# The last product of an attention takes over the tokens without neighbours, and an expert's result takes its weight and bias in one pass

## The chip, the cores and the metric

The kernel runs on one NeuronCore of a Trainium2 chip. The metric is the device time of one execution in microseconds (us); the figures given are medians of three runs. The engines are named as in the profile: PE (TensorE matmul), PEld (TensorE weight load), DVE (VectorE), ACT (ScalarE), POOL (GpSimd), SP (SyncE, which here issues DMAs).

## The reference

Two layers of a graph network on 2708 tokens of 256 numbers, with a 0/1 matrix `adj` of 2708 x 2708. Each layer is an attention over neighbours and a mixture of eight experts of which every token uses two, both with a residual:

```python
x = x + gnn0(layernorm(x), adj)     # masked softmax(q k' / 16) v, then elu
x = x + ffn0(layernorm(x))          # top 2 of 8 experts, hidden 1024, gelu
x = x + gnn1(layernorm(x), adj)     # below
x = x + ffn1(layernorm(x))          # top 2 of 8 experts, hidden 512, gelu

def gnn1(X, A):
    H = X @ W_fc + b_fc
    scores = (H @ w_att[:256])[:, None] + (H @ w_att[256:])[None, :] + b_att
    alpha = softmax(where(A > 0, scores, -1e9), axis=1)
    return alpha @ H
```

In `gnn1` the term of the row cancels in the softmax, so a token's result is a sum of `exp(s_k) * H_k` over its neighbours k, divided by the sum of `exp(s_k)`. A token without any neighbour gets, by the softmax of equal numbers, the plain mean over all 2708 tokens: the sum of all `H_k` divided by 2708. The same holds for layer 0.

## The kernel before

**Stages.** The profiled execution runs attention 0 (to about 525 us), the 45 chunks of experts 0 (to 863 us), attention 1 (to 1044 us), the 47 chunks of experts 1 (to 1255 us), and a tail that reads the experts' two results per token back and writes the output. Tokens lie in 22 tiles: 21 of 128 rows and one of 20 (`NT`, `ROWS`, `TAIL` = 20). Four tiles make a block of 512 (`GROUP` = 4, `QUARTER` = 32).

**Attention 1** (`layer1_attention`). The tiles of queries are taken in groups of 6, 6, 4, 3 and 3 (`GROUPS`), each tile with a PSUM accumulator (`acc`, six buffers). In a group a loop goes over the tiles of keys, k = 0 to 21. For k < 21, `attend` multiplies the 0/1 mask (`m`, turned from one-byte to four-byte numbers by ACT two steps ahead, L685) with the keys' weighted values in two parts (`parts`, L713). For k = 21, the 20 last keys, the masks of four tiles lie one under another on the partitions in quarters of 32, and `tails` (a copy by ACT in `load_tails`, L676) is multiplied with `e_tail` (L719). In the first group (`keys_and_values`) the values are computed on the way (L641), with PE kept busy by 28 products of no use before it starts (`busy(PAUSE)`, L752).

After a group, `evict` copies each accumulator to `raw` in SBUF, DVE and ACT in turn (L739), and gives the tile's further work to a `Line`. A line starts a new tile every `gap` of its steps and lets every running tile do one step, that is, one piece up to its next `yield`. In attention 1 a step comes after each k, or after every second k in the groups of 3. Pieces of one tile: `over_sum` (L244 to L249: is the sum of weights zero, a sum of N in its place, reciprocal, add the sum of all values where it was zero); residual, logits and the statistics of the norm, whose power -0.5 POOL computes (L727, L730, L209 to L215); the normed row, twice in memory, as `row0` and `row1` of DROW = 258 numbers, with the token's number behind it (POOL, L959); the best two experts and their one-hot (L992 to L1013); an exponential by ACT (L1015); two small products that count places (L1018, L1019); the two weights and places (L1022 to L1035), and two indirect DMAs by POOL that scatter the rows to `disp` (L1038). Layer 0 has the same `route` with some differences. The sum of all values, `total`, comes from `all_sum` after the first group (L819, L231, L234, L238).

Order of work: in attention 1 and experts 1 PE, ACT and DVE run in the order in which the code issues them (`manual_schedule`); POOL is ordered by the code in the first group of attention 1, SP everywhere. In layer 0 a planner orders the instructions of PE, ACT, DVE and POOL.

**Experts** (`slots`). For every chunk of 128 rows: `turned` (rows onto columns, L1247, then xe by DVE in layer 0, L1251, by ACT in layer 1, L1257); `up` (a copy `bias2` of the output bias, L1263, by DVE in layer 0 and ACT in layer 1; products L1270; gelu by ACT, L1278); `down` of the chunk before (products L1286; `y` = product + bias2, L1292; `y` times the row's weight, L1293; an indirect DMA by POOL into `xd`, which adds in layer 0, L1304, and only writes in layer 1, L1297). Between the products of `down` and `y`, `fetch` issues what the chunk three places later needs: its weights by an indirect DMA of POOL (L1199) and its rows by a DMA of SP (L1214). A row of weights already in place is given an index out of bounds and nothing is moved. In layer 0 an adding DMA past chunk 24 waits until the one before has landed. After chunk 44 (`OFTEN` = 45) the number of chunks is read and further ones run behind a branch (L1361, L1368).

The line goes on in experts 1 with two steps a chunk: the last tiles of attention 1 are routed there.

Of the kernel before, what the change touches and what calls it, by code (L numbers as in the profile page):

```python
# [9 lines left out]
F32 = mybir.dt.float32  # L10
I32 = mybir.dt.int32
# [26 lines left out]
assert TAIL <= QUARTER  # L38
# [31 lines left out]
def adj_ffn_kernel(ctx: ExitStack, tc: tile.TileContext, a: dict, out: bass.AP):  # L70
# [170 lines left out]
    def over_sum(raw, r, n, total):  # L241

        z = small.tile([P, 3], F32, name="z")
        nc.vector.tensor_scalar(z[:r, 0:1], raw[:r, n : n + 1], 0.0, None, ALU.is_equal)  # L244
        nc.vector.scalar_tensor_tensor(
            z[:r, 1:2], z[:r, 0:1], float(N), raw[:r, n : n + 1], op0=ALU.mult, op1=ALU.add
        )
        nc.vector.reciprocal(z[:r, 2:3], z[:r, 1:2])
        nc.vector.scalar_tensor_tensor(  # L249
            raw[:r, :n], total[:r], z[:r, 0:1], raw[:r, :n], op0=ALU.mult, op1=ALU.add  # L250
        )
        return z[:r, 2:3]
# [47 lines left out]
    def layer0_attention(line):  # L300
        with ExitStack() as scope, ExitStack() as until_last:
# [207 lines left out]
            def finish(t, raw, total):  # L509
                r, xr = ROWS[t], xin.pop(t)  # L510
                rinv = over_sum(raw, r, D, total)
                nc.vector.scalar_tensor_tensor(
                    raw[:r, :D], raw[:r, :D], rinv, bv_b[:r], op0=ALU.mult, op1=ALU.add
                )
                neg = rows0.tile([P, D], F32, name="neg", bufs=2)
                nc.vector.tensor_scalar(neg[:r], raw[:r, :D], 0.0, None, ALU.min)
                nc.scalar.activation(neg[:r], neg[:r], AF.Exp)
                yield
                nc.vector.scalar_tensor_tensor(
                    neg[:r], neg[:r], -1.0, raw[:r, :D], op0=ALU.add, op1=ALU.max  # L520
                )
                x1 = rows0.tile([P, D], F32, name="x1")
                nc.vector.tensor_add(x1[:r], neg[:r], xr[:r])
                yield from experts0.route(t, x1)
# [78 lines left out]
    def layer1_attention(mTs, kept, line, first_masks):  # L603
        with ExitStack() as scope:
# [63 lines left out]

            tails, converted_last = {}, [None]

            def load_tails(ts_):

                tails.clear()
                for b in sorted({t // GROUP for t in ts_}):
                    tails[b] = pool.tile([P, P], F32, name="m_tail")
                    nc.scalar.copy(tails[b], mTs[b][:, NT - 1, :P])  # L676
# [28 lines left out]
            def attend(ts_, k, accs):  # L705
                if k == GROUP:
                    load_tails(ts_)
                masks = next(masks_of_keys) if k < NT - 1 else None
                for t, acc in zip(ts_, accs):
                    r, j = ROWS[t], t % GROUP  # L710
                    if masks:
                        for i in range(2):
                            nc.tensor.matmul(  # L713
                                acc[:r], masks[t], parts[:, k, i],
                                start=(k == 0 and i == 0), stop=False,
                            )
                        continue
                    keys = slice(j * QUARTER, j * QUARTER + TAIL)
                    nc.tensor.matmul(  # L719
                        acc[:r, : VALUES + 1], tails[t // GROUP][keys, :r], e_tail[keys], start=False, stop=True  # L720
                    )

            def finish(t, raw, total):
                r, x2 = ROWS[t], kept[:, t]
                rinv = over_sum(raw, r, VALUES, total)
                yield
# [9 lines left out]
            def evict(ts_, accs, total):  # L736
                for j, (t, acc) in enumerate(zip(ts_, accs)):
                    raw = rows.tile([P, VALUES + 1], F32, name="raw", bufs=6)
                    (nc.scalar.copy if j % 2 else nc.vector.tensor_copy)(  # L739
                        raw[: ROWS[t]], acc[: ROWS[t], : VALUES + 1]  # L740
                    )
                    line.add(finish(t, raw, total))

            def keys_and_values(ts_, accs):
# [14 lines left out]
                for i in range(-3, NT + LAG1 - 1):  # L759
                    if i + 3 < NT:  # L760
                        stats[i + 3] = norm_begin(i + 3)
# [14 lines left out]
                    if 0 <= i < NT:  # L776
                        nc.vector.tensor_reduce(
                            sums_of[:, :, i], xT.pop(i)[:, :, : ROWS[i]], AX.X, ALU.add
                        )

# [4 lines left out]
            g0, total, beginning = 0, None, None  # L785
            for g, wide in enumerate(GROUPS):
# [30 lines left out]
                if g == 0:  # L817
                    sums = pool.tile([P, DC], F32, name="sums", bufs=1)
                    nc.vector.tensor_reduce(sums, sums_of, AX.X, ALU.add)  # L819
                    total = all_sum(pool, sums, wfc, VALUES, "total1")  # L820
# [3 lines left out]
                evict(ts_, accs, total)  # L824
# [42 lines left out]
    class Experts:  # L867
# [64 lines left out]
        def route(self, t, x, logits=None):  # L932
# [5 lines left out]
            rows2 = [  # L938
                routing.tile([P, DROW], F32, name=f"row{j}") if own_norm
                else kept_pool.tile([P, DROW], F32, name=f"row{j}", bufs=6)  # L940
                for j in range(2)
            ]
# [8 lines left out]
            if own_norm:  # L951
                xt = rows.tile([P, D], F32, name="xn", bufs=4)[:r]
                normed(xt, x[:r], mean, once)
                normed(rows2[0][:r, :D], x[:r], mean, twice)
            else:
                xt = rows2[0][:r, :D]
                row = normed(xt, x[:r], mean, once)
            for j in range(2):
                index = nc.gpsimd.tensor_copy(  # L959
                    rows2[j].bitcast(I32)[:r, D : D + 1],  # L960
                    token[:r, 0 if own_norm else j, t : t + 1],
                )
                if not own_norm:

                    tc.add_manual_dep(
                        index.ins, row.ins.name,
                        mybir.DependencyInfo(
                            mybir.DependencyClass.Sync, mybir.DependencyReason.DATA
                        ),
                        reason="no sooner than the row",  # L970
                    )
            if own_norm:
                nc.vector.tensor_copy(rows2[1][:r, :D], rows2[0][:r, :D])
            yield
            if not own_norm:
                (nc.vector.tensor_copy if self.begun else nc.scalar.copy)(
                    rows2[1][:r, :D], rows2[0][:r, :D]
# [45 lines left out]
            for j in range(2):  # L1023
                nc.vector.tensor_scalar(
                    rows2[j][:r, D + 1 : D + 2], p[:r, j : j + 1], den[:r, 1:2], None, ALU.mult
                )
# [9 lines left out]
            for j in range(2):  # L1036
# [3 lines left out]
                        rows2[j][:r], None,  # L1040
# [156 lines left out]
        def fetch_weights(self, s):  # L1197
            w, packed = self.ring[s % RING], self.packed_weights[0]
            nc.gpsimd.indirect_dma_start(  # L1199
# [3 lines left out]
            )  # L1203
            return w
# [34 lines left out]
        def slots(self, two, ps_mm, ps_tp, ps_acc, line):  # L1239
# [20 lines left out]
            def up(w, xe):  # L1260

                bias2 = two.tile([P, D], F32, name="bias2", bufs=2 if own_norm else 4)
                (nc.vector.tensor_copy if own_norm else nc.scalar.copy)(bias2, w[:, b2:b1])  # L1263
# [19 lines left out]
            def down(s, w, xg, hT, bias2, then):  # L1283
# [8 lines left out]
                nc.vector.tensor_add(y, ps, bias2)  # L1292
                nc.vector.tensor_scalar(y, y, xg[:, D + 1 : D + 2], None, ALU.mult)  # L1293
# [13 lines left out]
                if s < FULL_AFTER[self.early]:  # L1307
                    tc.declare_no_dep(start.ins, group=self.groups[3], reason="other rows of xd")
                    tc.add_to_no_dep_group(self.groups[2], start.ins)

# [5 lines left out]
            def slot(s, s1):  # L1316
# [4 lines left out]
                hT, bias2 = up(w, xe)  # L1321
# [5 lines left out]
                def fetch():  # L1327
# [4 lines left out]
                    if s + AHEAD < SLOTS and s + AHEAD == len(self.fetched):  # L1332
                        self.fetched.append((self.fetch_weights(s + AHEAD), self.fetch_rows(s + AHEAD)))
# [7 lines left out]
                if behind is None:  # L1341
                    fetch()
                else:
# [121 lines left out]
```

## Time and profile before

| what | value |
|---|---|
| median of three runs | 1288.06 us (1287.43 to 1289.81) |
| the profiled execution's own time | 1287.64 us |
| its span, first to last instruction | 1285.9 us |
| PE busy | 1200.1 us |
| DVE, ACT, POOL busy | 551.0, 439.9, 420.2 us |

The profile is of one execution. Its rows give start and duration of instructions in us from the span's start; in a row, brackets hold the idle time of the engine before it and what ended it. "sum, times, longest" stands in the view of waits. In the view by stage each engine's busy time in a stretch is followed by the number of instructions, and PEclk is the share of the TensorE clock that was granted.

### The profile page before, as it was taken

How to read it: one execution, taken by the hardware profiler on the slowest of the kernel's cores; microseconds unless marked ns; L12 is line 12 of the kernel's file. 1: busy time of each engine (PE TensorE's matmuls, PEld its weight loads, DVE VectorE, ACT ScalarE, POOL GpSimd, SP SyncE). 2: the span in 40 equal slices, each digit the busy share in tenths (PEclk: the TensorE clock that was granted, in tenths of full speed). 3: DMA queues.
4: the chain of work that ended last, by engine and by line, in shares of the span. 5: the costliest groups of instructions: out<-in, count | busy, mean ns of one | idle time of the engine just before them, and what ended most of it. 6: DMA issues, size and time to landing. Idle time of an engine off the chain costs nothing. (4 is left out here: it accounts for less than half of the span.)

```text
span 1285.9 us, 20986 instructions
## 1 busy us (share of the span) xinstructions
PE 1200.1 (93%) x7136; PEld 967.9 (75%) x7136; DVE 551.0 (43%) x2087; ACT 439.9 (34%) x1301; POOL 420.2 (33%) x538
## 2 busy tenths in 40 slices
PE   7999999999999999899999999999999888799980
PEld 4776666566656666699999999988998877799870
DVE  6623843633634526541212212116867775222114
ACT  3222222122112212433233232325766546444430
POOL 4100110110120113243333343335635457455550
PEclk9999999999999999999999999999999979899995
DMA  8701364997955905456657845433005125544358
GB/s 268 227 1 64 111 180 120 248 245 169 257 136 136 194 23 234 182 159 176 200 156 254 298 120 175 110 100 89 2 18 197 44 58 194 159 141 147 122 177 263
DMA packets 107242, 197.83 MB, mean 154 GB/s; under 512 B 26753, under 2 KB 81718, under 8 KB 100986
## 3 DMA queue, kind: packets, MB, share of 16 engines
q1 hardware_dynamic: 77276, 110.09, 30.8%
q0 software_dynamic: 27040, 83.56, 20.6%
q10 hardware_dynamic: 2814, 2.77, 0.7%
q8 instruction: 59, 0.97, 0.3%
q14 instruction: 53, 0.43, 0.1%
HBM read 263.63 MB, written 66.12 MB: 256 GB/s over the span
## 5 line engine op out<-in xcount | busy, mean ns | idle before, releaser
L1270 PE MATMUL mm<-xe,ring 128*128 128x128 f32 x2192 | 274.4, 279 | 17.7 <-ACT xe L1257 12.6
L1270 PEld LDWEIGHTS mm<-xe,ring 128*128 128x128 f32 x2192 | 264.9, 194 | 33.1 <-ACT xe L1257 14.9
L1286 PE MATMUL acc<-ring,hT 128*128 128x256 f32 x1096 | 267.7, 382 | 4.7 <-ACT hT L1278 3.0
L1278 ACT ACTIVATE hT<-mm,ring 128x128 f32<-128x128 f32 x548 | 156.5, 369 | 295.9 <-issue 191.9
L1286 PEld LDWEIGHTS acc<-ring,hT 128*128 128x128 f32 x1096 | 196.0, 192 | 25.7 <-ACT hT L1278 3.6
L504 PE MATMUL acc<-v,p 128*128 128x257 f32 (+1 forms) x880 | 209.1, 389 | 0.0
L447 PE MATMUL s<-g,xnT 128*128 128x512 f32 x420 | 206.3, 606 | 2.4 <-DVE mT L459 2.3
L1292 DVE TENSOR_TENSOR y<-acc,bias 128x256 f32<-128x256 f32 x92 | 39.0, 424 | 367.2 <-PE acc L1286 349.3
L504 PEld LDWEIGHTS acc<-v,p 128*128 128x128 f32 (+1 forms) x880 | 153.3, 190 | 18.1 <-issue 0.8
L1199 POOL DMA_INDIRECT ring<-L_ffn_packed,weight_row x98 | 103.4, 1055 | 183.0 <-issue 101.5
L1038 POOL DMA_INDIRECT disp<-row,to x88 | 88.2, 1002 | 147.6 <-issue 52.8
L713 PE MATMUL acc<-parts,m 128*128 128x266 f32 x924 | 130.5, 300 | 1.5 <-DVE raw L739 1.1
L215 POOL TENSOR_TENSOR ln_rs<-ln_rs,minus_half 128x2 f32<-128x2 f32 x88 | 66.5, 758 | 195.1 <-DVE ln_rs L211 175.9
L459 DVE TENSOR_SCALAR mT<-s 128x512 fp8e4<-128x512 f32 x105 | 71.9, 687 | 131.2 <-ACT p L458 131.1
L713 PEld LDWEIGHTS acc<-parts,m 128*128 128x128 f32 x924 | 120.5, 191 | 7.7 <-ACT m L685 2.6
L458 ACT ACTIVATE p<-s 128x512 f32<-128x512 f32 x105 | 62.1, 595 | 165.1 <-PE s L453 164.2
L447 PEld LDWEIGHTS s<-g,xnT 128*128 128x128 f32 x420 | 75.4, 191 | 49.0 <-issue 41.9
L1304 POOL DMA_INDIRECT xd<-y,xg x45 | 71.1, 1580 | 88.6 <-issue 32.2
L453 PEld LDWEIGHTS <-apart 128*128 128x128 fp8e4 x420 | 32.7, 99 | 61.2 <-issue 61.2
L685 ACT CAST m<-mT 128x512 fp32r<-128x512 fp8e4 (+4 forms) x168 | 71.0, 472 | 9.0 <-PE acc L713 6.3
L334 DVE TENSOR_SCALAR apart<-adj 128x677 fp8e4<-128x677 int32 x80 | 40.7, 511 | 53.1 <-DMA adj<-in_adj_dram 52.6
L1297 POOL DMA_INDIRECT xd<-y,xg x47 | 47.3, 1007 | 24.8 <-PE tp L1247 9.1
(228 smaller groups left out, 1154.5 us busy)
## 6 DMA issues: line engine op xcount, KB each, us to landing
adj<-in_adj_dram SPq DMA_DIRECT2D x84, 338.5 KB
L_ffn_packed<-in_L_ffn_W_dram SPq DMA_DIRECT2D x16, 1024.0 KB
xg<-disp SPq DMA_DIRECT2D x98, 129.0 KB
L_ffn_packed<-in_L_ffn_W_dram SPq DMA_DIRECT2D x16, 512.0 KB
neighbours<-mT SPq DMA_DIRECT2D x5, 1408.0 KB
mT<-neighbours SPq DMA_DIRECT2D x5, 1408.0 KB
xin<-in_x_dram SPq DMA_DIRECT2D x42, 128.0 KB
ring<-L_ffn_packed SPq DMA_DIRECT2D x4, 1154.0 KB
```

Source lines behind the costliest of these rows:

```text
L215: nc.gpsimd.tensor_tensor(rs[:r, 1], rs[:r, 0], minus_half[:r], ALU.pow)
L447: nc.tensor.matmul(ps[:kr, :nb], xnT[:, c, k0 : k0 + kr], g[:, c, :nb], start=(c == 0), stop=False,)
L459: nc.vector.tensor_scalar(mT[:kr, k, :], ps[:kr, :nb], -BIG / 2, None, ALU.is_gt, saturate=False,)
L504: nc.tensor.matmul(accs[j][:r], p[keys, q0 : q0 + r], v[keys, k, :], start=(k == 0), stop=(k == NT - 1),)
L685: nc.scalar.copy(m[:, : q1 - q0], mTs[b][:, k, q0 - b * BN : q1 - b * BN])
L713: nc.tensor.matmul(acc[:r], masks[t], parts[:, k, i], start=(k == 0 and i == 0), stop=False,)
L1038: nc.gpsimd.indirect_dma_start(disp[:], bass.IndirectOffsetOnAxis(ap=to[:r, j : j + 1], axis=0), rows2[j][:r], None,)
L1199: nc.gpsimd.indirect_dma_start(w, None, packed[:], bass.IndirectOffsetOnAxis(ap=self.weight_row[:, s : s + 1], axis=0), bounds_check=E * P ...
L1270: nc.tensor.matmul(ps[:, i, :], w[:, c * hidden + f * P : c * hidden + (f + 1) * P], xe[:, c, :], start=(c == 0), stop=(c == DC - 1),)
L1278: nc.scalar.activation(hT[:, f, :], ps[:, i, :], AF.Gelu, bias=w[:, b1 + f : b1 + f + 1])
L1286: nc.tensor.matmul(ps, hT[:, f, :], w[:, w2 + f * D : w2 + (f + 1) * D], start=(f == 0), stop=(f == hc - 1),)
L1304: start = nc.gpsimd.indirect_dma_start(xd[:], at, y, None, bounds_check=N - 1, oob_is_err=False, compute_op=ALU.add)
```

## The change

Six things change.

1. **Tokens without neighbours.** Layer 0 leaves for each tile a column of 0/1 in `alone` (1 where the token has no neighbour). In attention 1 `over_sum` is gone: the last product gets one more key, row 20 of each quarter. Its mask is `alone`, its value the sum of all values, its weight N. The columns are copied into `rows_alone` (DVE, `load_alone`, at k = 0), turned by PE (a transpose into a buffer of `misc`) and joined to the tail masks by DVE in `load_tails` at k = 4, in place of ACT's copy. `place`, nine small DVE operations, makes the two 0/1 columns that say which partitions are keys and which the one behind. The sum of all values is computed in `sum_of_all` inside the first group, and added to `e_tail` by two DVE operations. `finish` takes the reciprocal alone and has one `yield` fewer.
2. **Evictions of attention 1.** ACT takes the first two of three, DVE the third.
3. **Two rows in one tile.** `row0` and `row1` become `row[:, 0]` and `row[:, 1]`. In layer 1 one POOL copy writes both token numbers (two before); in both layers one DVE operation writes both weights (two before).
4. **Scaled bias.** `bias2` is the bias times the row's weight, made in `up`; `y` is then one DVE operation, product times weight plus `bias2`.
5. **Layer 0, chunk 44.** `down` of chunk 43 is issued whole, and the fetch for chunk 47 after it; the weights' DMA on POOL waits until the adding DMA has landed.
6. `over_sum` in layer 0 writes its 0/1 column to `alone` instead of a column of `z`.

```diff
+    alone = const.tile([P, NT], F32, name="alone")
+    nc.gpsimd.memset(alone, 0.0)
-    def over_sum(raw, r, n, total):
+    def over_sum(raw, r, n, total, alone):
-        nc.vector.tensor_scalar(z[:r, 0:1], raw[:r, n : n + 1], 0.0, None, ALU.is_equal)
+        nc.vector.tensor_scalar(alone, raw[:r, n : n + 1], 0.0, None, ALU.is_equal)
...
+            place = pool.tile([P, 4], F32, name="place", bufs=1)
+            in_tail, behind_tail = place[:, 2:3], place[:, 3:4]
...
+            rows_alone = [
+                pool.tile([P, P], F32, name=f"alone{i}", bufs=1) for i in range(DC)
+            ]
+            for x in rows_alone:
+                nc.gpsimd.memset(x, 0.0)
+            def load_alone(ts_):
+                for b in sorted({t // GROUP for t in ts_}):
+                    n = len(BLOCKS[b][2])
+                    nc.vector.tensor_copy(
+                        rows_alone[b % DC].rearrange("p (j n) -> p j n", j=GROUP)[:, :n, TAIL],
+                        alone[:, b * GROUP : b * GROUP + n],
+                    )
             def load_tails(ts_):
...
-                    nc.scalar.copy(tails[b], mTs[b][:, NT - 1, :P])
+                    ps = misc.tile([P, GROUP, P], F32, name="misc")
+                    nc.tensor.transpose(ps[:, 0, :], rows_alone[b % DC], ident)
+                    nc.vector.scalar_tensor_tensor(
+                        tails[b], mTs[b][:, NT - 1, :P], in_tail, ps[:, 0, :],
+                        op0=ALU.mult, op1=ALU.add,
+                    )
...
-                    keys = slice(j * QUARTER, j * QUARTER + TAIL)
+                    keys = slice(j * QUARTER, j * QUARTER + TAIL + 1)
...
-            def finish(t, raw, total):
+            def finish(t, raw):
                 r, x2 = ROWS[t], kept[:, t]
-                rinv = over_sum(raw, r, VALUES, total)
-                yield
+                z = small.tile([P, 2], F32, name="z")
+                rinv = z[:r, 1:2]
+                nc.vector.reciprocal(rinv, raw[:r, VALUES : VALUES + 1])
...
-                    (nc.scalar.copy if j % 2 else nc.vector.tensor_copy)(
+                    (nc.vector.tensor_copy if j % 3 == 2 else nc.scalar.copy)(
...
+            def sum_of_all():
+                ps = misc.tile([P, GROUP, P], F32, name="misc").rearrange("p g n -> p (g n)")
+                for c in range(DC):
+                    nc.tensor.matmul(
+                        ps[:, :VALUES], sums_wide[:, c, :], wfc[:, c, :VALUES],
+                        start=(c == 0), stop=(c == DC - 1),
+                    )
+                nc.vector.scalar_tensor_tensor(
+                    e_tail[:, :VALUES], ps[:, :VALUES], behind_tail, e_tail[:, :VALUES],
+                    op0=ALU.mult, op1=ALU.add,
+                )
...
                 for i in range(-3, NT + LAG1 - 1):
+                    if i == NT:
+                        sum_of_all()
...
-                    sums = pool.tile([P, DC], F32, name="sums", bufs=1)
-                    nc.vector.tensor_reduce(sums, sums_of, AX.X, ALU.add)
-                    total = all_sum(pool, sums, wfc, VALUES, "total1")
...
-            for j in range(2):
-                nc.vector.tensor_scalar(
-                    rows2[j][:r, D + 1 : D + 2], p[:r, j : j + 1], den[:r, 1:2], None, ALU.mult
-                )
+            nc.vector.tensor_scalar(
+                rows2[:r, :, D + 1 : D + 2], p[:r, :2].unsqueeze(2), den[:r, 1:2], None, ALU.mult
+            )
...
-            def up(w, xe):
+            def up(w, xe, factor):
...
-                (nc.vector.tensor_copy if own_norm else nc.scalar.copy)(bias2, w[:, b2:b1])
+                if own_norm:
+                    nc.vector.tensor_scalar(bias2, w[:, b2:b1], factor, None, ALU.mult)
+                else:
+                    nc.scalar.activation(bias2, w[:, b2:b1], AF.Copy, scale=factor)
...
-                nc.vector.tensor_add(y, ps, bias2)
-                nc.vector.tensor_scalar(y, y, xg[:, D + 1 : D + 2], None, ALU.mult)
+                nc.vector.scalar_tensor_tensor(
+                    y, ps, xg[:, D + 1 : D + 2], bias2, op0=ALU.mult, op1=ALU.add
+                )
...
+                elif own_norm and s == OFTEN - 1:
+                    added = down(*behind, lambda: None)
+                    fetch(added)
```

## The prediction

> **What bounds the kernel now.** I read the page first, then busy time by stage, then who PE waits for in attention 1, then the timelines of the engines it waits for.
>
> ```profile
> span 1285.9 us, 20986 instructions
> ...
> 941.00:977.00 36.00, 33.26 (x275) 32.28 (x273) 25.70 (x140) 21.82 (x61) 15.19 (x31) 1.00 0.09 31
> 977.00:1000.60 23.60, 23.60 (x185) 22.94 (x185) 19.76 (x108) 14.31 (x40) 13.73 (x23) 0.93 0.76 256
> 1000.60:1047.00 46.40, 39.01 (x281) 34.33 (x281) 36.39 (x197) 23.39 (x87) 25.56 (x39) 0.91 0.20 59
> 1047.00:1099.00 52.00, 38.95 (x243) 34.56 (x243) 29.30 (x152) 31.64 (x77) 33.36 (x42) 0.89 0.39 131
> ```
>
> PE comes first after the stretch's length. Elsewhere it is busy almost throughout (1200.1 of 1285.9 us), and there a shorter instruction of DVE or ACT buys nothing. It idles 2.7 us in the second group of attention 1 (941 to 977), 7.4 in the last two groups and the passage to experts 1 (to 1047), and 13.1 while experts 1 begins. So the edits in attention 1 are what can count. PE's waits from 935 to 1047 us:
>
> ```profile
> PE misc L1018 <- DVE sel L1013: 3.6, 4, 1.4
> PE tp L1247 <- issue: 2.2, 1, 2.2
> PE misc L1059 <- DVE seen L1029: 1.9, 1, 1.9
> PE misc L1018 <- DVE hot L1006: 1.8, 1, 1.8
> PE acc L713 <- DVE raw L739: 1.1, 2, 0.9
> ```
>
> PE waits for routing on DVE, which is late although it isn't full. DVE's waits from 940 to 1047 us name its cause, and the timelines of DVE and of POOL show one turn of it:
>
> ```profile
> DVE row L219 <- POOL ln_rs L215: 17.3, 13, 2.0
> ```
> ```profile
> 961.87 0.41 DVE L219 TENSOR_SCALAR row<-kept,ln_mv,ln_rs 128x256 f32<-128x256 f32 x1 [1.54 <-POOL ln_rs L215]
> 962.20 0.15 DVE L244 TENSOR_SCALAR z<-raw 128x1 f32<-128x1 f32 x1
> ...
> 963.05 0.15 DVE L1022 RECIPROCAL den<-den 128x1 f32<-128x1 f32 x1
> 963.24 0.34 DVE L1024 TENSOR_SCALAR row<-p,den 128x1 f32<-128x1 f32 x2
> ...
> 963.89 0.17 DVE L1035 TENSOR_REDUCE to<-hot 128x2 int32<-128x16 f32 x1
> ...
> 967.97 0.41 DVE L219 TENSOR_SCALAR row<-kept,ln_mv,ln_rs 128x256 f32<-128x256 f32 x1 [1.54 <-POOL ln_rs L215]
> ```
> ```profile
> 964.86 1.04 POOL L1038 DMA_INDIRECT disp<-row,to  x1 [2.20 <-DVE p L1003]
> 966.20 0.98 POOL L1038 DMA_INDIRECT disp<-row,to  x1 [0.30 <-issue]
> 967.20 0.73 POOL L215 TENSOR_TENSOR ln_rs<-ln_rs,minus_half 128x2 f32<-128x2 f32 x1
> ```
>
> It is a ring through two engines. Normed row to `over_sum` 0.33 us; `over_sum` 0.85 (962.20 to 963.05); weights and places 1.01 (to 964.06); 0.80 until POOL issues; two scatters 2.32; the next tile's power, queued behind them, 0.75; 0.04 to DVE's next normed row. That is 6.10 us a tile, and 967.97 - 961.87 is 6.10. PE needs less: with six tiles, three k of twelve products of 0.124 us (L713: 12 in 1.49 us on the chain) are 4.5 us; with three tiles, six k of six are also 4.5. PE runs ahead until it needs `sel`, then waits.
>
> **The change, part by part.**
>
> *Ring in attention 1.* `over_sum` leaves it (-0.85); a bare reciprocal (0.16, row L248) comes with the residual, beside POOL's scatters. The second weight operation starts 0.13 after the first (L1024 x2 lasts 0.34, one 0.21): -0.13. New ring 5.12 us. One step fewer moves a tile's whole routing one step forward, with its three products or copies, two scatters and the power on POOL; their order between tiles stays, because steps of neighbouring tiles are three apart before and after. One POOL copy of a token number goes (two last 0.31), but POOL idles there: 0.
>
> In the second group six turns at 6.1 are 36.6 us, more than PE's 33; at 5.12 they are 30.7 and PE leads. The 2.7 idle us shrink to about 0.2: -2.5. In the last two groups seven tiles are scattered, six turns between them: 6 x 0.98 = 5.9; one eviction fewer on DVE there (L739, 0.35 to 0.4) helps too, but PE's own 4.5 begins to bind, so I take -5.5 (3 to 8: the stretch's 7.4 idle us and its reduced clock bound it above).
>
> *Clock.* Behind the gaps of the second group PEclk is 0.93 for 23.6 us in which PE never idles: 1.65 us lost. [...] I follow the trace, -1.65[...].
>
> *Last product.* Eight transposes on PE. The row (two L225 in 0.22 us on the chain) gives 0.11 each, 0.9 together; they fall on PE's path where it is full: two in the first group, two in the second, one in the third, three in the ring-bound groups. The buffer of `misc` may have to wait: in the first group the second transpose comes right behind the values of a tile (L641), whose buffer ACT frees about 1 us later. Bounds 0.2 and 1.2 there: I take 0.7, plus 0.3 for the next two groups. DVE's joining (bound by L976's copy 0.28 and L727's 0.48) replaces ACT's L676 (0.30), at k = 4, needed at k = 21: 17 products of k cover it; without them it would cost 0.4 x 8. The copies of `load_alone` (eight, about 0.2 each) lie at k = 0, four k ahead. One more row in the product: [...] 0. `place`, nine DVE operations of some 0.2, falls before the first norms (DVE is idle 8.9 us up to 872.49), and PE's idle products run until 877.53: 0; uncovered it would be 1.8. POOL's memsets lie there too.
>
> *Sum and evictions.* The four passes of L234 (1.10 on the chain) move forward in PE's order: 0. Before, DVE had to copy `total` and add to the logits before its first eviction, and PE waited 0.87 for it at 940.67. Now ACT evicts the first accumulator while the last tails are multiplied: -0.9. ACT's extra evictions (0.38 each) delay mask casts, which are two k ahead: 0. Where experts 1 begins, PE's 2.2 us wait ends with DVE's two evictions; one goes to ACT: -0.4.
>
> *Result in one pass.* `y` was 0.42 + 0.35 with a start 0.46 later; one pass from PSUM is 0.42 (L1292) to 0.48 (L727): about -0.35 in latency. Inside a row of chunks PE's next 3.7 or 7.3 us cover it: 0. It counts at two ends. After experts 0, PE's restart at 865.21 waits for DVE's branch, which stands behind `y`: -0.35. At the end, y, scatter, read back, output form one chain: -0.35. `bias2` gets 0.05 to 0.1 dearer on ACT or DVE, beside PE: 0. One risk is a table: as ACTIVATE Copy it runs between gelus. Rows here show Copy with a pointer scale only between exponentials (L648, 0.48, no load); none shows it beside gelu. If it needed its own table, two loads of 1.28 (the row of L1278's ACT_TABLE_LOAD) would come with each of 47 chunks. [...]
>
> *Chunk 44 of layer 0.* POOL now issues the adding DMA at about 859.9 in place of 861.44; then the fetch, which waits for its landing, and the last add behind the fetch (1.05 + 0.30). Before, the last add at 866.01 waited for the landing too. It comes at about 865.3, 0.7 earlier; SP's rows are only issued in another place. But attention 1 starts behind PE's idle products, with the first norm ready at 874.64: 0 either way, up to 2.9 us.
>
> *Layer 0.* `over_sum` keeps its four operations; one fewer L1024 per tile is off PE's path. The planner may reorder: 0, within 3 either way, as PE's gaps in attention 0 sum to some 10.
>
> **Sum.** Profiled time 1287.64 (span 1285.9 and 1.74 around it) - 2.5 - 5.5 - 1.65 + 1.0 - 0.9 - 0.4 - 0.35 - 0.35 = 1277.0. The median lay 0.42 above the profiled execution: 1277.4.
>
> **The rivals.** *A, the sum:* 0.62, 1277.4, by its bounds 1271 to 1283.
>
> *B, given back:* the last tiles still pass through experts 1, where ACT changes tables eleven times (1.28 each) and POOL is busy 33 of 52 us. Coming earlier then only lengthens waits there; half is kept, 1283 (1281 to 1286). For: that stretch idles 13 us with the same work left. Against: its waits are PE's for ACT, on work that isn't moved. 0.23.
>
> *C, nothing:* ring and transposes cancel, 1287 to 1290. 0.08.
>
> *D, slower:* the transposes, in PE's order, wait for a buffer of `misc` that routing holds until DVE frees it (L1028). Five calls of `load_tails`; each can wait a lag of DVE, at most a turn, 5.1 us. It decides from (10.7 + 2.6) / 5 = 2.7 us a call; at 3.2 the time is about 1293. For: PE meets DVE's lag at L1018 already. Against: k = 4 comes before most routing products of a group. 0.07, with the table load (2.6 x 47, less PE's slack of 1 us: +70) and a worse order in layer 0 inside it.
>
> **How the numbers follow.** 0.2% (2.6 us) is about what a measurement of this kernel can tell from no change. Faster: A and most of B, 0.84; same 0.08; slower 0.08. The range 1270 to 1287 takes in A and B.
>
> **What would show it.** Normed rows (L219's successor) 5.1 us apart in the second group; waits of L1018 on `sel` mostly gone; DVE about 17 us less in attention 1; no drop of PEclk behind 977; PE's restart after experts 0 at 864.9; no ACT_TABLE_LOAD beyond the present ones. Waits of PE on DVE at the new transposes would speak for D; a shorter attention 1 with a longer beginning of experts 1 for B.

## The result, and the profile after

The changed kernel took 1279.51 us beside 1289.78 us for the kernel before (medians of 14 runs each on one chip): a ratio of 0.9926, 95% interval 0.9909 to 0.9944, or 9.5 us less by this ratio (the two medians lie 10.3 us apart). On another chip, in the experiments, the ratio was 0.9947 (0.9924 to 0.9969), 6.8 us less. The forecast, 0.9917 of the time before, lies inside the first interval and just under the second.

The profiled execution took 1282.53 us, with a span of 1280.7. Its busy time by stage (a stretch, its length, busy time of PE, PEld, DVE, ACT and POOL with the number of instructions, PEclk, DMA share, GB/s). The rows are the second, the third and the last two groups of attention 1, then attention 1 with the passage to experts 1, then experts 1:

```profile
943.00:976.70 33.70, 33.66 (x281) 32.83 (x279) 22.95 (x127) 23.11 (x63) 15.30 (x22) 1.00 0.10 37
976.70:999.00 22.30, 22.30 (x186) 21.71 (x186) 16.62 (x90) 14.58 (x40) 12.61 (x22) 1.00 0.73 267
999.00:1038.60 39.60, 36.90 (x286) 33.16 (x282) 30.17 (x165) 23.63 (x85) 22.77 (x30) 0.96 0.21 65
...
868.00:1042.70 174.70, 166.87 (x1212) 154.00 (x1212) 124.75 (x569) 108.71 (x329) 97.23 (x147) 0.99 0.22 74
1042.70:1250.50 207.80, 189.24 (x1231) 171.92 (x1231) 42.43 (x159) 101.38 (x302) 109.20 (x113) 0.95 0.46 147
```

In the second group PE is busy for all of its 33.7 us, and the stretch is as long as PE's work. The last two groups keep 2.7 us of idle time. Experts 1 still idles 18.6 us. What PE waits for from 938 to 1043 us (the waits of 0.6 us and more; one of 0.5 is left out):

```profile
PE tp L1316 <- issue: 2.9, 1, 2.9
PE misc L1080 <- DVE sel L1075: 2.1, 1, 2.1
PE misc L707 <- DVE m_tail L708: 0.6, 1, 0.6
```

Before, PE waited 3.6 us in four places for `sel`, with 1.8 more for its one-hot (`hot`) and 1.9 for the counts (`seen`). One wait for `sel` is left, in the last groups. New is L707, the transpose that waits for a `misc` buffer; this one, too, lies in the last groups. The wait on entering experts 1 has grown from 2.2 to 2.9 us. The ring itself, on DVE and on POOL, in the second group:

```profile
957.19 0.41 DVE L219 TENSOR_SCALAR row<-kept,ln_mv,ln_rs 128x256 f32<-128x256 f32 x1 [1.42 <-POOL ln_rs L215]
957.52 0.15 DVE L1084 RECIPROCAL den<-den 128x1 f32<-128x1 f32 x1
957.71 0.23 DVE L1085 TENSOR_SCALAR row<-p,den 128x2 f32<-128x2 f32 x1
...
962.31 0.41 DVE L219 TENSOR_SCALAR row<-kept,ln_mv,ln_rs 128x256 f32<-128x256 f32 x1 [1.33 <-POOL ln_rs L215]
...
967.43 0.41 DVE L219 TENSOR_SCALAR row<-kept,ln_mv,ln_rs 128x256 f32<-128x256 f32 x1 [1.32 <-POOL ln_rs L215]
```
```profile
964.33 1.03 POOL L1099 DMA_INDIRECT disp<-row,to  x1 [1.36 <-DVE p L1065]
965.67 0.98 POOL L1099 DMA_INDIRECT disp<-row,to  x1 [0.30 <-issue]
966.67 0.73 POOL L215 TENSOR_TENSOR ln_rs<-ln_rs,minus_half 128x2 f32<-128x2 f32 x1
```

The reciprocal of `den` now follows the normed row after 0.33 us; the four operations of `over_sum` between them are gone. The turn is 962.31 - 957.19 = 5.12 us, where it was 6.10. The same ring runs on, 0.98 us shorter.

It sets the pace up to the middle of the last two groups only. There the seven steps from one normed row to the next took 4.65, 6.10, 6.09, 6.76, 6.87, 7.98 and 6.22 us before, and take 3.88, 5.70, 5.10, 5.11, 7.13, 7.08 and 7.12 now: the first four are 3.8 us shorter together, the last three 0.3 longer.

### The profile page after: what moved, and what is told of

It reads as the page before. It is cut to its first block, busy times and chain, and to the rows that moved or that the text cites. A ratio compares the mean times of both kernels' runs of the same rounds, so it can differ in the third digit from the quotient of the medians.

```text
span 1280.7 us, 20738 instructions
## 1 busy us (share of the span) xinstructions
PE 1202.6 (94%) x7144; PEld 967.6 (76%) x7144; DVE 514.0 (40%) x1906; ACT 444.9 (35%) x1298; POOL 414.3 (32%) x519
## 5 line engine op out<-in xcount | busy, mean ns | idle before, releaser
L1343 PEld LDWEIGHTS mm<-xe,ring 128*128 128x128 f32 x2192 | 260.9, 196 | 37.5 <-issue 17.6
L1359 PE MATMUL acc<-ring,hT 128*128 128x256 f32 x1096 | 260.6, 382 | 1.6 <-ACT hT L1351 1.1
L1359 PEld LDWEIGHTS acc<-ring,hT 128*128 128x128 f32 x1096 | 198.9, 191 | 23.7 <-ACT hT L1351 1.3
L1365 DVE SCALAR_TENSOR_TENSOR y<-acc,xg,bias 128x256 f32<-128x256 f32 x92 | 44.4, 483 | 402.2 <-PE acc L1359 386.4
L750 PE MATMUL acc<-parts,m 128*128 128x266 f32 x924 | 127.7, 295 | 0.0
L720 ACT CAST m<-mT 128x512 fp32r<-128x512 fp8e4 (+4 forms) x168 | 71.8, 474 | 12.4 <-PE acc L750 7.2
```

Of the source, the lines that this page charges most:

```text
L720: nc.scalar.copy(m[:, : q1 - q0], mTs[b][:, k, q0 - b * BN : q1 - b * BN])
L750: nc.tensor.matmul(acc[:r], masks[t], parts[:, k, i], start=(k == 0 and i == 0), stop=False,)
L1343: nc.tensor.matmul(ps[:, i, :], w[:, c * hidden + f * P : c * hidden + (f + 1) * P], xe[:, c, :], start=(c == 0), stop=(c == DC - 1),)
L1359: nc.tensor.matmul(ps, hT[:, f, :], w[:, w2 + f * D : w2 + (f + 1) * D], start=(f == 0), stop=(f == hc - 1),)
```

## Experiments

Each ratio is against runs of the kernel before on the same chip in the same session. That kernel's own median ran from 1276.8 to 1291.1 us between chips, so only ratios are compared.

**1 and 2: the change in two halves.** a1 has the edits of attention 1 and the `alone` column. a2 has the rest: rows in one tile, scaled bias, chunk 44.

```diff
 a1: + load_alone, place, sum_of_all, reciprocal in finish, new order of evictions
     (rows in two tiles, y in two passes, chunk 44 as before)
 a2: + rows2[:r, 1, :] and one weight operation, bias2 * factor, y in one pass, chunk 44
     (over_sum and its yield kept)
```

> The kernel before with the edits of attention 1 alone (one more key in the last product, sum of all inside the first group, evictions two of three by ACT; layer 0 only writes its 0/1 column elsewhere). Ring theory: nearly the whole gain, 8 to 10 us of the 10; normed rows 5.25 us apart in the second group (the second weight operation is still there, 0.13). Rival, that fewer instructions per expert chunk and per routed row make the gain: under 3 us.

> The kernel before with the other edits alone: two rows in one tile, scaled bias and result in one pass, chunk 44 of layer 0. Ring theory: -0.7 us at the two ends and 0.13 us a turn (5.97 in place of 6.10), some 1 to 2 us together. Rival: 5 us or more. If layer 0 itself has become slower by these edits (the profiled execution after came 3.6 us later to the end of experts 0 than the one before), it shows here as a later end of experts 0, and not in the kernel with the attention's edits alone.

Measured: a1 0.9969 (0.9953 to 0.9986), some 4.0 us; a2 0.9979 (0.9964 to 0.9994), some 2.7 us. Both halves pay, and their product, 0.9948, is about the whole. Run 2 was also to show whether the other edits slow layer 0: its experts 0 ended at 869.3 us, run 1's at 871.2, so nothing speaks for that. The row turn was 5.25 us in a1 and 5.98 in a2. Attention 1 with the passage, as one row of the view by stage of each, a1 first:

```profile
871.20:1045.70 174.50, 165.48 (x1212) 152.78 (x1212) 126.11 (x586) 108.53 (x329) 98.84 (x163) 0.99 0.23 74
```
```profile
869.30:1049.10 179.80, 168.16 (x1202) 154.56 (x1202) 131.64 (x589) 108.00 (x332) 96.50 (x144) 0.98 0.22 71
```

So a1 has the whole saving of the stage (182.4 before, 174.7 with everything, on another chip), and yet its time fell by 4 and not by the 8 to 10 expected. Some of what attention 1 saves does not reach the end. That is the question of the later runs.

**3: the ring's step without the computation.** In b the kernel before loses only the `yield` behind `over_sum`, so `over_sum` runs beside POOL's work while all its operations stay.

```diff
                 rinv = over_sum(raw, r, VALUES, total)
-                yield
```

> The kernel before with one yield removed: over_sum keeps its four operations but is done in the piece of the residual and the norm's statistics, beside POOL's scatters and no longer between the normed row and the weights. Ring theory: what counts is its place. The turn falls from 6.10 to about 5.3 to 5.6 (DVE's work behind the places, 3.4 us, then lasts a little longer than POOL's 3.1), and 3 to 6 us of the time go. Rival, that DVE's amount of work counts: no change, as not an instruction is saved.

The turn fell as expected, 970.66 - 965.14 = 5.52 us (rows of DVE's timeline):

```profile
965.14 0.41 DVE L219 TENSOR_SCALAR row<-kept,ln_mv,ln_rs 128x256 f32<-128x256 f32 x1 [0.84 <-POOL ln_rs L215]
...
970.66 0.42 DVE L219 TENSOR_SCALAR row<-kept,ln_mv,ln_rs 128x256 f32<-128x256 f32 x1 [0.84 <-POOL ln_rs L215]
```

The time did not: 1.0008 (0.999 to 1.0027). Attention 1 with the passage took 178.2 us, 4 to 5 less than in two profiles of the kernel before (182.4 and 183.3, on other chips), and of this nothing arrived at the end. PE's waits in the first 24 chunks of experts 1 are one hint of where it may have gone:

```profile
PE mm L1269 <- DMA ring<-L_ffn_packed,weight_row: 4.5, 2, 2.5
PE mm L1269 <- ACT xe L1256: 4.1, 5, 1.1
```

PE waits 4.5 us there for the DMAs of weights. What the kernel before has in that place, runs 5 and 6 show. But this profile cannot settle it: it came to the end of experts 0 only at 875.7 us, 4 to 6 us after the three others of this chip (871.2, 869.3 and 870.3), with PE's instructions of layer 0 in the same order as in the kernel before, and this execution took 2.9 us more than b's median. Where b's saving was lost stays open.

**4: the old order of the evictions.** c is the changed kernel with `nc.scalar.copy if j % 2 else nc.vector.tensor_copy`.

> The changed kernel with evictions in turn as before, DVE first. If ACT's evictions are worth what the prediction says: PE waits again at the start of the second group, but less than 0.9 us since the copy of the total is gone from DVE (0.3 for the addition to the logits and 0.4 for the eviction), and 0.4 where experts 1 begins: 0.5 to 1.5 us slower than the changed kernel. Rival: the order of evictions is worth nothing, the same time within 0.5 us.

Measured 0.9952 (0.9932 to 0.9972), without a run of the changed kernel on that chip. Its second group took 33.8 us, the changed kernel's 33.7. Where that group begins, PE waited 0.87 us for the first eviction in the kernel before and 0.17 here; in the changed kernel it doesn't wait. So the new order is worth some 0.2 us there, and the other 0.7 came from the sum of all values being done earlier, which leaves DVE no copy of `total` to make first. What the order is worth in the whole time this run doesn't tell, since no direct comparison was made.

**5 and 6: both kernels profiled on one chip.**

> The kernel before once more, for a second table by stage. Theory (the gain is the ring's): the row turn of the second group of attention 1 is again near 6.1 us, its groups two to four take again some 37, 24 and 43 us. Rival (the difference of the first two profiles was the luck of one execution): these three stages come out like the changed kernel's, 33.6, 22.4 and 39.5. If the clock dip behind 977 us was no accident, the third group shows it again and takes 25 us; without it 23. The stop of 5 to 7 us on TensorE near 1090 us is there again if it belongs to the kernel.

> The changed kernel on this chip. Theory: 0.991 to 0.994 of the kernel before, as the sum of its two halves (0.9969 and 0.9979 give 0.995). Rival (the old order of evictions was the better one): it comes out slower than 0.995, where the kernel with the old order stood. Row turn of the second group 5.1 us, third and fourth group 22.4 and 39.5.

The changed kernel: 0.9947 (0.9924 to 0.9969). Turns were 6.10 and 5.12 us again. The second, the third and the last two groups took 37.2, 23.6 and 46.0 us in the kernel before and 33.6, 22.4 and 39.5 in the changed one, so the first pair's difference was not the luck of one execution. Attention 1 with the passage, then experts 1, in the kernel before and in the changed one:

```profile
865.50:1048.80 183.30, 169.39 (x1201) 155.32 (x1201) 133.22 (x604) 107.89 (x332) 97.41 (x160) 0.97 0.22 70
1048.80:1242.90 194.10, 181.35 (x1233) 166.68 (x1233) 61.28 (x237) 96.72 (x302) 111.49 (x119) 0.99 0.48 157
```
```profile
863.90:1037.40 173.50, 166.51 (x1211) 153.78 (x1211) 124.47 (x566) 109.13 (x329) 97.09 (x147) 0.99 0.22 74
1037.40:1234.60 197.20, 182.15 (x1231) 166.28 (x1231) 42.93 (x163) 101.81 (x302) 109.36 (x113) 0.99 0.48 155
```

Attention 1 is 9.8 us shorter and experts 1 is 3.1 us longer. Why, PE's waits in its first 24 chunks tell; the kernel before, then the changed one:

```profile
PE mm L1270 <- ACT xe L1257: 5.6, 7, 1.0
PE mm L1270 <- DMA ring<-L_ffn_packed,weight_row: 1.4, 2, 1.2
```
```profile
PE mm L1343 <- ACT xe L1326: 5.5, 7, 1.1
PE mm L1343 <- DMA ring<-L_ffn_packed,weight_row: 4.9, 3, 2.0
```

The waits for `xe` are the same. Those for the weights' DMAs grew by 3.5 us, about what experts 1 lost. That POOL has the same scatters and fetches to issue in 9.8 us less, and so the weights do not come that much earlier, is argued; no row here times it. And the first pair of profiles does not show it. There the same waits, before and after, are

```profile
PE mm L1270 <- DMA ring<-L_ffn_packed,weight_row: 1.6, 1, 1.6
```
```profile
PE mm L1343 <- DMA ring<-L_ffn_packed,weight_row: 1.5, 3, 1.0
```

and experts 1 took 0.8 us longer (207.0 to 207.8) with PE busy 2.9 us longer at a lower clock (PEclk 0.96 and 0.95). Both executions of that pair were stopped for 6.7 to 6.9 us in this stretch (last section), which may have given the weights time.

The expected clock dip behind 977 us was not there in the second profile of the kernel before (PEclk 1.00 from 977.4 to 1001.0 us), nor was the stop of 5 to 7 us near 1090 (PE's longest wait in the first 24 chunks is 1.2 us).

**7: fewer idle products.** d is the changed kernel with `PAUSE = 20` in place of 28.

> The changed kernel with 20 idle products in place of 28 between the end of experts 0 and the first transposes of attention 1. Theory (the transition is hidden behind the idle products, so taking chunk 44's work early was worth nothing): the first norm is ready 2.2 us before TensorE is through with its idle products, so this saves 1.5 to 2.2 us against the changed kernel (0.9983 of it). Rival (the norms set the restart already): no difference, 0 +- 0.3, and the first transposes wait for the norm rather than for the idle products.

Measured 0.9936 (0.9914 to 0.9958); against 0.9947 for the changed kernel on this chip no difference can be told. The first group fell from 75.0 to 73.4 us and PE's busy time in it from 73.3 to 70.6, and PE now waits for the first norm:

```profile
PE misc L225 <- DVE xn L219: 0.9, 1, 0.9
```

So with 28 products the norms are covered, by an estimated 1.8 us (the 2.7 us of work that went, less the wait of 0.9). Experts 1 took 200.2 us instead of 197.2:

```profile
1035.60:1235.80 200.20, 185.93 (x1231) 171.14 (x1231) 42.62 (x161) 101.45 (x302) 109.71 (x113) 0.97 0.47 152
```

This looks like a second saving returned to the weights, and it isn't. In the first 24 chunks PE's waits for weights grew from 4.9 to 5.8 us while those for `xe` fell from 5.5 to 3.2; over the whole of experts 1 PE idled 14.3 us in place of 15.1. But PE was busy for 185.9 us in place of 182.2, at PEclk 0.97 in place of 0.99: what was lost here was lost to the clock.

**8: no table changes in experts 1.** In e the routing of tiles that come during experts 1 uses Copy in place of Exp: their exponential is left out.

```diff
-            nc.scalar.activation(p[:r, :k], p[:r, :k], AF.Exp, accum_out=den[:r, 0:1])
+            nc.scalar.activation(p[:r, :k], p[:r, :k],
+                AF.Copy if self.begun and not own_norm else AF.Exp, accum_out=den[:r, 0:1])
```

> The changed kernel where the routing of the tiles that come during experts 1 takes Copy in place of Exp (the exponential of their weights is left out), so ScalarE loads no table there. Rival B (what attention 1 gains is given back in the first third of experts 1, to ScalarE's tables): the waits of the products for xe in the first 50 us shrink and the time falls by 3 to 6 us against the changed kernel. Theory (experts 1 is bound by TensorE and its weights, the tables lie beside them): 0 to 2 us faster.

Measured 0.9928 (0.9907 to 0.9949), not separable from the changed kernel. PE's waits in the same chunks:

```profile
PE mm L1346 <- DMA ring<-L_ffn_packed,weight_row: 4.5, 4, 2.3
...
PE mm L1346 <- ACT xe L1329: 1.6, 2, 1.1
```

In experts 1 ACT has 292 instructions in place of 302 and is busy 88.5 us in place of 101.8; ten table loads of 1.28 us would be 12.8 of these 13.4, by estimate. PE's waits for ACT in the first 24 chunks fell from 5.5 to 1.6 us, those for the weights stayed, and experts 1 took 196.9 us in place of 197.2. Of the 3.9 us less of waits the clock took back 1.7 over the whole of experts 1 (PE was busy 183.8 us in place of 182.2, PEclk 0.97 in place of 0.99), and longer waits for rows and weights the rest (PE idled 13.1 us in place of 15.1). So the weights' waits remain (4.5 us) when the table loads are gone by that count, and taking the tables out gains nothing that can be told; that the tables cost nothing by themselves is not shown.

**9 and 10: half the bytes of the weights, in both kernels.** Each fetch in experts 1 brings half a row, and of other weights; the products are unchanged.

```diff
-                w, None, packed[:],
+                w[:, : w.shape[1] // 2] if half else w, None,
+                packed[:].rearrange("r (h c) -> (r h) c", h=2) if half else packed[:],
```

> The kernel before where each fetch of a weight set in experts 1 brings half a row (and of other weights): half the bytes, the products unchanged. Theory (weights arrive in time in the kernel before but for some 1.4 us of TensorE's waits in the first 24 slots): 1 to 3 us faster, 0.998 to 0.999 of the kernel before. Rival (experts 1 is not touched by its weights at all): no difference.

> The changed kernel with the same halved fetches. Theory (of the 9 to 10 us that attention 1 loses some 3 to 4 are given back in experts 1, because its weights do not come 9 us earlier): TensorE's waits for the ring of weights, 4.9 us in the first 24 slots, go, and it is 9 to 11 us under the halved kernel before, 0.989 to 0.991 of the whole kernel before. Rival (the difference of experts 1 between the kernels is chance, or the give-back lies in the passage and the tables): the waits go in both alike, the difference to the halved kernel before stays 6 to 8 us.

Measured 0.9956 (0.9939 to 0.9973) and 0.986 (0.9829 to 0.9891). PE's waits in the first 24 chunks, kernel before first:

```profile
PE mm L1272 <- ACT xe L1259: 10.0, 6, 5.3
PE mm L1272 <- issue: 3.5, 1, 3.5
```
```profile
PE mm L1345 <- ACT xe L1328: 7.1, 6, 2.5
PE mm L1345 <- ACT hT L1353: 2.2, 2, 1.2
```

No wait for the ring of weights is left in either. With half the bytes the change is worth 0.0096 of the time, about 12.4 us, in place of 0.0053 to 0.0074. The direction is the theory's. The size decides nothing: the two intervals together leave some 4.6 us either way (only five executions of run 10 were timed), which takes in the theory's 9 to 11 us and the rival's 8. Nor do the waits decide, since the rival expected them to go in both as well. And in these profiles the kernel before was stopped (last section; 5.3 us of its waits for `xe`) and the changed kernel was not, which favours the change.

**11 and 12: the edits together.** g has 20 idle products, the old order of evictions, and late exponentials as a power on POOL. i has the first two alone.

```diff
-PAUSE = 28
+PAUSE = 20
...
+            if self.begun and not own_norm:
+                nc.gpsimd.tensor_tensor(p[:r, :k], e_const[:r, :k], p[:r, :k], ALU.pow)
...
+                nc.vector.tensor_reduce(den[:r, 0:1], p[:r, :k], AX.X, ALU.add)
```

> The changed kernel with what the earlier runs point to: 20 idle products, the old order of the evictions, and the exponential of the late tiles as a power on POOL (e to the p, summed on VectorE), so that ScalarE keeps one table in experts 1. Theory: attention 1 loses 1.8 us by the idle products and 1 in its last group by the evictions, the waits for xe lose 2 to 4, half of it is given back to the weights: 2 to 4 us under the changed kernel, 0.990 to 0.993. Rival (experts 1 is bound by the arrival of its weights): all is given back, 0.994 to 0.995 as the changed kernel.

> The changed kernel with 20 idle products and the old order of evictions, the exponential left on ScalarE as it was: the combined kernel without its power on POOL. Theory (the power on POOL is what cost the combined kernel its gain): the last group is back at 21.4 to 22.5 us from 26.6, and the kernel is at 0.991 to 0.995 of the kernel before. Rival (the two other edits do not go together): the last group stays at 26 us and the kernel at 0.998. As to the evictions alone: if the old order is the better one in the last group, that group takes 21.4 us again and not 22.5.

g gave 0.9984 (0.9969 to 0.9999), worse than the changed kernel; i gave 0.9945 (0.9927 to 0.9962), its equal. The last two groups, with the sum of the stage, in g and in i:

```profile
1001.70:1045.40 43.70, 36.89 (x282) 33.09 (x282) 31.52 (x168) 23.38 (x78) 27.09 (x33) 0.96 0.20 59
```
```profile
995.70:1034.20 38.50, 35.48 (x282) 31.89 (x282) 30.78 (x168) 23.92 (x84) 21.93 (x29) 1.00 0.21 64
```

The last two groups are 5.2 us longer in g. One row of its POOL, and PE's wait for `sel` from the second group to the passage:

```profile
1027.45 1.68 POOL L1080 TENSOR_TENSOR p<-e_const,p 128x8 f32<-128x8 f32 x1
1029.11 0.69 POOL L217 TENSOR_TENSOR ln_rs<-ln_rs,minus_half 128x2 f32<-128x2 f32 x1
```
```profile
PE misc L1085 <- DVE sel L1077: 6.2, 2, 3.1
```

The power of 128 x 8 takes 1.68 us and stands ahead of the next tile's power in the ring. Two of them fall into the last two groups, 3.4 us, and a third into the passage; PE's wait for `sel` is 6.2 us where i has 2.4. That is 3.8 of the 5.2 us; the other 1.4 are the clock's (PE busy 36.9 us in place of 35.5, PEclk 0.96 in place of 1.00). In i the last groups are 1.0 us shorter than the changed kernel's 39.5 (runs 6 and 12), but PE is busy 1.3 us less there at PEclk 1.00 in place of 0.96, so this is the clock and not the evictions, and the entry to experts 1 grew from 3.0 to 4.5 us. No version was found that is shown to beat the changed kernel.

## Why the prediction was right, and where not

The forecast called a gain of 10.6 us in the profiled execution. From the end of experts 0 to the end of the program the change saved 8.8 us in the first pair of profiles (423.2 to 414.4) and 8.6 in the second (411.3 to 402.6). What came before that (layer 0) differed by +3.6 and -0.8 us, no steady difference. Term by term, the first pair and then the second:

| step | predicted | measured |
|---|---|---|
| ring turn, second group | 6.10 to 5.12 | 6.10 to 5.12, both |
| first group (1.1 of L234 moved in, 0.7 for transposes) | +1.8 | +1.7, +0.3 |
| second group (-2.5, -0.9, -1.1 moved out, +0.15) | -4.35 | -3.4, -3.6 |
| third group (clock -1.65, +0.15) | -1.5 | -2.7, -1.2 |
| last two groups | -5.5 | -4.0, -6.5 |
| passage to experts 1 | -0.4 | +0.7, +1.2 |
| attention 1 in all | -9.95 | -7.7, -9.8 |
| experts 1 | 0 | +0.8, +3.1 |
| PE's restart after experts 0 | -0.35 | -0.8, -0.8 |
| end | -0.35 | -1.1, -1.2 |

The measured column cuts the second group from the third at 975.6 us, the prediction at 977.0. Between the two lie 1.1 us of idle time that the prediction counts into the second group and the table into the third. With it moved, the forecasts are -3.25 and -2.6.

**Ring.** The working was right to 0.01 us in the turn, and the second group became PE's: 33.6 to 33.7 us are PE's work there without any gap. In the last two groups the number came out within its bounds of 3 to 8, but not by the six turns of 0.98 that it was made of: the steps listed above are 3.55 us shorter in sum, and the last three did not shrink. What sets their 7.1 us stays open.

**Evictions.** The -0.9 at the start of the second group came, but the reason given (ACT evicts first) is worth 0.2 of it; 0.7 came from the copy of `total` that no longer stands ahead (run 4).

**Passage.** The -0.4 was wrong in sign. PE's wait there does not end with the evictions, as the step assumed: it grew by 0.7 to 1.1 us when PE came earlier, and in i by another 1.3 when PE came earlier still. What PE waits for the profile does not name ("issue"); that it is bound to something that does not move with PE is all that these rows show.

**Clock.** The step took the loss behind 977 us for one that the gaps cause and the change removes. In the first pair the size was right: of the third group's -2.7 us, 1.1 are the idle time and 1.6 the clock (PE busy 23.9 us before and 22.3 after, PEclk 0.93 and 1.00). In the second pair there was no dip to remove there (PEclk 1.00 in both), and its -1.2 is the idle time alone. (The second profile of the kernel before has its dip at the start of the first group instead, PEclk 0.50 from 865.5 to 867.5 us and 0.75 in the two us behind, which is why that row shows +0.3 and not +1.7.) As a cause the gaps alone are not enough. The two profiles of the kernel before have the same gaps ahead of 977 (1.36 and 0.90 us; 1.35 and 0.89), and only the first has the dip:

```profile
976.00:980.00 4.00, 3.26 (x16) 3.20 (x16) 3.79 (x21) 3.78 (x13) 2.55 (x3) 0.63 0.53 112
980.00:984.00 4.00, 4.00 (x33) 4.00 (x32) 1.87 (x11) 1.32 (x4) 2.59 (x5) 0.94 0.95 365
```
```profile
978.00:982.00 4.00, 3.51 (x29) 3.44 (x29) 3.79 (x18) 3.97 (x13) 2.74 (x3) 1.00 0.60 123
```

So the trace's reading, that these gaps cost 1.65 us, does not hold in each execution. The dip here is worth 0.37 x 4 + 0.06 x 4 = 1.7 us by the two rows. Why it came in one execution and not in the other is not shown.

**Transposes and rival D.** Two transposes waited for a `misc` buffer, 0.44 and 0.56 to 0.58 us, 1.0 in all. Rival D's mechanism exists, but at 0.2 us a call of `load_tails` where it needed 2.7 to decide. The first lies in the first group, as foreseen, the other in the last groups.

**Result in one pass.** The two ends were mis-sized. PE's wait at the restart, on DVE's branch, in the kernel before and after:

```profile
PE acc L752 <- DVEq L1368: 2.4, 1, 2.4
```
```profile
PE acc L810 <- DVEq L1449: 1.6, 1, 1.6
```

That is 0.8 us against the 0.35 taken from the two durations. It belongs to the edits of run 2 (run 1 still waits 2.4 us, run 2 1.6); whether to the one pass or to the new order in chunk 44 was not set apart. At the end, the last scatter starts 0.80 us after PE's last product in place of 1.13, as predicted, but the first read-back 0.40 earlier and the ninth 0.85 earlier (8.60 in place of 9.45). The rest is thus gained in the read-back and was not foreseen.

**Zeros.** No table was loaded for ACTIVATE Copy: 20 ACT_TABLE_LOADs before and after. `bias2` got 0.10 us dearer on ACT (428 to 530 ns) and 0.07 on DVE (284 to 349), as expected. The last product took a mean of 424 ns with 20 rows (L719) and with 21 (L756), so the one more row cost nothing. Chunk 44 was worth 0, but not as worked out: the last add came 3.24 us after PE's end before and 3.30 after, not 0.7 earlier. The idle products cover it either way (run 7). "DVE about 17 us less in attention 1" was wrong: 133.4 to 124.8 is 8.6 us, since `place`, the joining of tails (2.7 us), the copies of `alone` and the two sums came in.

**Rival B.** On the second chip it stands between the sum and the measurement: of 9.8 us saved in attention 1, 3.1 were returned in experts 1. The rival named ACT's tables and POOL. The waits of runs 5 and 6 put it with the arrival of the weights, and run 8 leaves these waits (4.5 us) when the tables are gone; the halved fetches of runs 9 and 10 agree but don't decide, and the first pair shows no such return. At half kept the rival was too dark; the sum, at nothing returned, too bright. That the forecast's total came out near was partly luck: attention 1 gave 0.2 to 2.2 us less than its sum, and experts 1 took back 0.8 to 3.1 us where nothing was counted, while the restart and the end gave 1.9 to 2.0 us where 0.7 was.

## What to carry to other kernels

Where a routing ring through two engines sets the pace, take an operation out of the ring rather than off a busy engine. Here the turn followed to a hundredth of a microsecond, but it counts only until the next engine's own work fills the stage (here PE's 33.7 us in the second group). Then look at the stage behind: in one of two pairs of profiles a third of the saving turned into waits for the DMAs of weights (1.4 to 4.9 us). Before a saving is said to be returned, split the stage into PE's idle time and its busy time with the granted clock: in run 7 it was the clock (PEclk 0.97 in place of 0.99). And don't move work onto the ring's other engine: two powers of 1.7 us on POOL cost 3.8 us of waits, and a lower clock came on top (PEclk 0.96 in place of 1.00).

## What was not expected of the hardware

Nearly the same gap was followed by a dip of the clock in one run and not in another. In the last groups the changed kernel's gap of 2.15 us (1024.66 to 1026.81 us) was followed by one in run 6 (first fence), while run 4's gap of 2.13 us at the same place (1031.37 to 1033.50) was not (second):

```profile
1024.00:1026.00 2.00, 0.66 (x6) 0.43 (x5) 1.86 (x14) 0.00 (x0) 1.06 (x1) 1.00 0.02 4
1026.00:1028.00 2.00, 1.19 (x10) 1.07 (x10) 1.86 (x11) 1.55 (x9) 1.39 (x3) 0.99 0.61 138
1028.00:1030.00 2.00, 2.00 (x11) 1.79 (x11) 0.81 (x4) 1.25 (x5) 1.79 (x3) 0.50 0.80 218
```
```profile
1031.00:1033.00 2.00, 0.37 (x3) 0.15 (x2) 1.83 (x14) 0.00 (x0) 1.10 (x1) 1.00 0.10 13
1033.00:1035.00 2.00, 1.50 (x12) 1.37 (x12) 1.86 (x9) 1.86 (x10) 1.65 (x2) 1.00 0.65 145
1035.00:1037.00 2.00, 2.00 (x19) 1.87 (x17) 0.83 (x5) 1.18 (x5) 1.80 (x3) 1.00 0.80 224
```

What sets the two apart is not shown.

ACT and DVE also stop together in experts 1 in some executions. In run 9 both resume within 0.04 us, released by something that the trace does not name:

```profile
1104.24 1.28 ACT L1280 ACT_TABLE_LOAD   x1 [5.09 <-remote]
```
```profile
1104.28 0.17 DVE L1061 COPY n_e<-misc 128x8 f32<-128x8 f32 x1 [4.41 <-remote]
```

The first profile of the kernel before has it at the same point (6.73 and 5.60 us). The first profile of the changed kernel and run 11 have stops of ACT of 6.92 and 7.65 us at other points of experts 1, each with stops of DVE beside it (of up to 3.94 and 4.23 us); the other ten profiles have none. Its cause stays open.
